# A pre-norm attention and FFN block on one core: the order of weight preparation at the start, the warming products and the power instructions

## The chip, the cores and the metric

One core of a Trainium2 chip runs the whole kernel. The metric is the device time of one execution in microseconds (us): the median before is 983.02 us of 4 runs (982.63 to 983.35). In the profile, PE is TensorE (PEld its weight loads), DVE is VectorE, ACT is ScalarE, POOL is GpSimd and SP is SyncE, which issues most DMAs. Each engine takes its own instructions in a fixed order; a wait at the head of an engine's queue holds all that stands behind it.

## The reference

Inputs are `x` of 8 x 512 x 256 floats, `gamma` (256), `w_qkv` (256 x 3072), `w_out` (1024 x 256), a router matrix (256 x 8) and the two FFN matrices (256 x 1024 and 1024 x 256) with biases. There are 16 heads of 64. Cut to what matters:

```python
xn  = rms_norm(_layernorm(x), gamma)          # x / norm * sqrt(256) * (gamma + 1)
q, k, v = split(xn @ w_qkv)                   # per head
attn = softmax((q * 64 ** -0.5) @ k.T)
x = x + (attn @ v) @ w_out
y = _layernorm(x)
combine = top-2 of softmax(y @ router_w), normalised
x = x + (gelu(y @ w1 + b1) @ w2 + b2) * sum(combine)
```

## The kernel before, in words

**Numbers in two halves.** Products run in 16-bit floats, but nearly to float accuracy: every operand is stored as a high part (the value cast to f16) and a low part (value minus high part, also f16), and every product is three products: high by high, low by high, high by low (`PARTS`, line 462). For weights, `split` (line 166) does this: ACT writes `hi` as a Copy with a scale factor, then DVE writes `lo` with one `scalar_tensor_tensor`. The scale factor is a power of two times `gamma + 1`. It is found from the weights themselves: ACT squares a weight tile with an accumulator (`square`, line 174), TensorE adds over the partitions with a matrix of ones (`total`, line 186, the tile `pn`), and DVE makes a power of two from the sum with shifts (`powers`, line 201); `with_gamma` (line 224) multiplies it by `gamma + 1`. For q and k, `find_qk` (line 231) returns `rest`, seven more small DVE instructions that give `ab`, the factors with which QT and KT are scaled after their product. The weights come as halves of 512 columns: q0, k0, v0, v1, q1, k1. 128 columns belong to a pair of heads, so that q0 and k0 hold the pairs 0 to 3.

**Start (lines 717 to 756).** x of the first batch element, gamma and the weights are loaded (lines 130 to 140); q1 and k1 go into the pool `stage` of four buffers, which the first four halves fill, so that SP waits for two of these to be read. TensorE runs 80 products of zeros (`warm`, line 720) from the start on. DVE finds the mean and variance of x, POOL raises to the powers -0.5 and 0.5 (`scale1`, lines 382 to 401), DVE normalises the four row tiles (`normalize`, line 413). ACT squares q0, k0 and v0; then come `pn`, the factors, the split of all 512 columns of q0 and k0, the transposes of the normalised x (`transpose_rows`, line 426; the tile `xnT`), `rest`, the squares of v1, and the projection of pair 0 (`project_qk`, line 490; the tile `pqk`), which ACT and DVE turn into QT and KT.

**Steps (lines 958 to 979).** A tile of scores is 128 rows of one pair of heads against all 512 keys: 256 such tiles in all, four for each pair, 8 pairs for each batch element. The loop goes over 128 double steps of two tiles each, so that a batch element takes 16. In each: TensorE makes the scores `ps` (`scores`, line 517); DVE takes the row maximum `mx`; ACT runs the exponential, four instructions `e<-ps`; ACT casts the high part `hl`; POOL subtracts the low part; SP issues a DMA that transposes both into `hT`; three double steps later (`LAG = 6` tiles) TensorE multiplies `hT` by VT (`weigh`, line 557; the tile `po`) and DVE divides (`divide`, line 577). Other work is put into the double steps by a table, `at(step, position, function, arguments)` (line 763): position "d" stands after the maxima and before the exponentials (and one step later than its number says), "a" makes a product whose high and low parts come after the exponentials, "e" comes after the exponentials and ahead of the parts of "a", "b" comes at the end of the step. Every second double step projects the next pair (QT and KT), the others make a tile of v (VT). The split of v (`split_wv`) stands in steps 0 and 1, the squares of q1 and k1 in "d" of step 1, their factors in step 3, their split (`split_qk1`) in steps 4 and 5, loads and squares of `w_out` and the router in steps 2 to 6, and their split in steps 11 to 16. `scale1`, `scale1_rest`, `scale1_last` and `normalize` for the next batch element stand in "d", on POOL but for a reciprocal. The order on each engine is as written out here.

After the attention of the last batch element come the FFN products of all elements (lines 984 to 1021); the change doesn't touch them.

Two lines that the steps of the prediction turn on:

```python
wqk = [const.tile([P, NC, 2, INNER], F16, name=f"wqk{i}") for i in range(2)]   # high and low parts of q and k
lows = [part_qk("q", 0, c) for c in range(NC)]                                 # c: the two halves of 128 input rows
```

Of the kernel before, what the change touches and what calls it, by code (L numbers as in the profile page):

```python
# [11 lines left out]
F32 = mybir.dt.float32  # L12
# [5 lines left out]
ALU = mybir.AluOpType  # L18
# [11 lines left out]
VW = 130  # L30
WARM = 80
EARLY = 6
HLB, HTB = 5, 7
SB = 4
XB = 4
# [41 lines left out]
def preln_block(  # L77
# [45 lines left out]
    def staged(name, src, eng, shape=(NC, 512)):  # L123
        t = stage.tile([P, *shape], F32, tag="stage", name=name)
        eng.dma_start(out=t, in_=src)
        return t
# [7 lines left out]
    for name, off, eng in (  # L134
        ("q0", 0, nc.scalar), ("k0", INNER, nc.sync), ("v0", 2 * INNER, nc.sync),
        ("v1", 2 * INNER + 512, nc.sync), ("q1", 512, nc.sync), ("k1", INNER + 512, nc.sync),
    ):
        raw[name] = staged(f"w_{name}", wqkv_r[:, :, off : off + 512], eng)
    for b in range(1, XB):
        load_x(b)  # L140
    w_r = const.tile([P, NC, NE], F32, name="w_r")
# [23 lines left out]

    def split(hi, lo, src, f):

        nc.scalar.activation(hi, src, AF.Copy, scale=f)
        return lambda: nc.vector.scalar_tensor_tensor(lo, src, f, hi, ALU.mult, ALU.subtract)
# [4 lines left out]
    def square(name, col, src, scale=1.0):  # L174

        pool, what = (hl_p, "hT") if name in ("qk0", "v") else (stage, "stage")
        junk = pool.tile([P, 1024], BF16, tag=what, name="junk", bufs=HTB if what == "hT" else SB)
        nc.scalar.activation(
            junk[:, 0 : src.shape[-1]], src, AF.Square, scale=scale,
            accum_out=sums[name][:, col[0], col[1] : col[1] + 1],  # L180
        )
# [41 lines left out]

    def with_gamma(name, s):

        f = stat.tile([P, 2, NC], F32, name=f"f_{name}")
        for i in range(2):
            nc.vector.tensor_scalar(f[:, i, :], gam1, s[:, i : i + 1], None, ALU.mult)
        return f

    def find_qk(half, n2):

        v = nc.vector
        added(n2)
        s, u, z = powers(f"qk{half}", n2)
        factors["qk", half] = with_gamma(f"qk{half}", s)

        def rest():  # L240
            ab = stat.tile([P, 2], U32, name=f"ab_{half}")
            w = stat.tile([P, 1], U32, name=f"w_{half}")
            v.tensor_copy(w, u[:, 1:2])
            v.tensor_tensor(z[:, 0:1], u[:, 0:1], w, ALU.add)
            v.tensor_scalar(z[:, 0:1], z[:, 0:1], 101, 254, ALU.add, ALU.min)
            v.tensor_scalar(w, z[:, 0:1], 1, None, ALU.logical_shift_right)
            v.tensor_tensor(u[:, 0:1], z[:, 0:1], w, ALU.subtract)
            v.tensor_scalar(ab[:, 0:1], u[:, 0:1], 23, None, ALU.logical_shift_left)
            v.tensor_scalar(ab[:, 1:2], w, 23, None, ALU.logical_shift_left)
            factors["out", half] = ab.bitcast(F32)  # L250

        return rest

    def find_v(n2):
        added(n2)
        s, u, z = powers("v", n2)
        factors["v"] = with_gamma("v", s)
        factors["1/v"] = inverses("v", u, z)
# [29 lines left out]
    with ExitStack() as att:  # L288
# [13 lines left out]
        VT = [work.tile([P, HEADS, VW], F16, tag=f"VT{r}", name=f"VT{r}") for r in range(NT)]  # L302

        wv = [work.tile([P, NC, INNER], F16, name=f"wv{i}") for i in range(2)]
        wo = [work.tile([P, NP, D], F16, name=f"wo{i}") for i in range(2)]
# [11 lines left out]

        def part_qk(n, half, c):
            i = "qk".index(n)
            hi, lo = (w[:, c, i, ts(half, 512)] for w in wqk)  # L320
            return split(hi, lo, raw[f"{n}{half}"][:, c], factors["qk", half][:, i, c : c + 1])

        def squares(name, i, key):
            for c in range(NC):
                square(name, (i, c), raw[key][:, c, :], gam1[:, c : c + 1])

# [9 lines left out]
        def split_qk1(n, c):  # L336
            part_qk(n, 1, c)()
            done("wqk")

        def split_wv(c, j):  # L340
            cols = ts(j, 512)
            f = factors["v"][:, j, c : c + 1]
            split(wv[0][:, c, cols], wv[1][:, c, cols], raw[f"v{j}"][:, c, :], f)()
            done("wv", j)
# [36 lines left out]

        def scale1(b, part):


            g = nc.vector if b == 0 else nc.gpsimd
            mv = norm1[b][0]
            if part == 0:
                rstd = tiny.tile([P, NT], F32, tag="rstd", name="rstd")
                g.tensor_scalar(rstd, mv[:, :, 1], LN_EPS, None, ALU.add)
                nc.gpsimd.tensor_tensor(rstd, rstd, halves[:, 0, :], ALU.pow)  # L390
                nm = tiny.tile([P, NT], F32, tag="nm1", name="nm1")
                g.tensor_scalar(nm, mv[:, :, 0], -1.0, None, ALU.mult)
                norm1[b] += [nm, rstd]
                return
            norm = tiny.tile([P, NT], F32, tag="norm", name="norm")
            g.tensor_scalar(norm, mv[:, :, 1], float(D), 1e-30, ALU.mult, ALU.max)
            nc.gpsimd.tensor_tensor(norm, norm, halves[:, 1, :], ALU.pow)
            _, nm, rstd = norm1[b]
            g.tensor_tensor(norm, norm, rstd, ALU.mult)
            g.tensor_scalar(norm, norm, NORM_EPS, float(D) ** -0.5, ALU.max, ALU.mult)  # L400
            norm1[b] = [nm, None, norm, rstd]
# [11 lines left out]
        def normalize(norm, b, t, tag):  # L413
# [5 lines left out]
            c = slice(t, t + 1)  # L419
            eng = nc.vector if (tag, b) == ("x", 0) else nc.gpsimd  # L420
            src = (xs if tag == "x" else x2)[b]
# [4 lines left out]
        def transpose_rows(b, c):  # L426

            if c == 0:
                xnT[b] = work.tile([P, NC, 2, S], F16, tag="xnT", bufs=2, name=f"xnT{b}")
            pt = bank("pt")  # L430
            need(NT, "xn", "x", b)
# [58 lines left out]
        def project_qk(pair, n):  # L490

            b, p = divmod(pair, NP)
            need(NC, "xnT", b)
            if p >= NP // 2:
                need(2 * NC, "wqk")
            pm = bank("pqk")
# [222 lines left out]

        warm = bank("warm")  # L720
        for i in range(WARM):
            nc.tensor.matmul(warm[:, 0:256], cold[:, 0:P], cold, start=True, stop=True)

# [5 lines left out]
        nc.vector.tensor_scalar_add(gam1, gam, 1.0)  # L729
        scale1(0, 0)  # L730
        scale1(0, 1)
        for name, k, m in (("qk0", 2, NC), ("v", 2, NC), ("qk1", 2, NC), ("o", 3, 1), ("w", 3, 2)):
# [5 lines left out]
        for t in range(NT):  # L738
            normalize(norm1, 0, t, "x")
        squares("v", 0, "v0")  # L740
        rest = find_qk(0, total("qk0"))
        parts = [transpose_rows(0, c) for c in range(NC)]
        lows = [part_qk("q", 0, c) for c in range(NC)]
        for high, _ in parts:
            high()
        lows += [part_qk("k", 0, c) for c in range(NC)]
        for _, low in parts:
            low()
        for low in lows:
            low()  # L750
        rest()
        squares("v", 1, "v1")
        for high, low in [project_qk(0, n) for n in range(2)]:
            high()
            low()
        lows = [find(find_v, "v")[1]]

# [36 lines left out]

        for c in range(NC):
            at(0, "e", split_wv, c, 0)
            at(1, "e", split_wv, c, 1)
            at(4, "e", split_qk1, "q", c)
            at(5, "e", split_qk1, "k", c)
        for i in range(2):  # L800
            at(1, "d", squares, "qk1", i, "qk"[i] + "1")
        at(3, "b", find_rest, find_qk, 1, "qk1")
        at(2, "d", load_small)
        for j in range(2):
            at(3 + j, "d", load_wo, j)
            at(5 + j, "d", square_wo, j)
        at(5, "d", square_wr)
        at(10, "b", find, find_o, "o")
# [12 lines left out]
        for b in range(B):  # L821
# [10 lines left out]
            if b + 1 < B:  # L832
                at(max(s0 - 5, 1), "d", scale1_rest, b + 1)
                at(s0 - 4 if b else 2, "d", scale1_last, b + 1)
                for t in range(NT):
                    at(s0 + 21 + 2 * t, "a", project, b, 1, t)
                    at(max(s0 - 9 + t // 2, 0), "d", sums1, b + 1, t)
                    at(s0 + (1 + t if b else 2 + t // 2), "d", normalize, norm1, b + 1, t, "x")
                at(max(s0 - 7, 0), "d", scale1, b + 1, 0)
                at(max(s0 - 6, 0), "d", scale1, b + 1, 1)  # L840
                if b + XB < B:
                    at(s0 + 33, "d", load_x, b + XB)
                for c in range(NC):
                    at(s0 + 6 + 2 * c, "b", transpose_rows, b + 1, c)
        del units[-2, "a"]
# [210 lines left out]
```

## Time and profile before

The profiled execution took 982.73 us; its span in the profile, from the first instruction to the last, is 980.6 us.

| What | us |
|---|---|
| median of 4 runs | 983.02 |
| the profiled execution | 982.73 |
| its span | 980.6 |
| squares of q0 and k0 begin on ACT (q0 has landed) | 8.11 |
| last warming product begins | 12.11 |
| `f_qk`, the factors of q0 and k0, ready | 14.31 |
| first product `pqk` of pair 0 | 16.79 |
| QT of pair 0 on ACT | 21.13 |
| first exponential, double steps 0, 1, 2, 3 | 25.00, 32.33, 41.99, 48.27 |
| double steps 4, 5, 6 | 52.44, 62.08, 70.35 |
| double steps 11, 16 | 100.41, 132.03 |

A row of the timeline has the start, the time from the start of the first to the end of the last of its instructions, the engine, the operation, what is written and read, and how many instructions are merged; in brackets the idle time of the engine before it and what ended that. Instructions of one engine overlap a little: of two in a row, the second starts before the first has wholly ended, so that the distance from start to start is smaller than one instruction's time. PEclk is the share of its full clock that TensorE was granted.

### The profile page before, as it was taken

What the parts mean: (1) busy time and instruction counts of PE and PEld (TensorE: products, weight loads), DVE (VectorE), ACT (ScalarE), POOL (GpSimd) and SP (SyncE); (2) the same over time, 40 slices, a digit from 0 to 9 for tenths busy, and PEclk for the clock granted to TensorE, in tenths of its full rate; (3) what the DMA queues carried; (4) which work ended last, traced back from release to release, by engine and by line L of the source; (5) the groups of instructions that cost most, each with busy time, mean ns of one, the idle gap of its engine ahead of it and who ended that gap; (6) DMA issues with size and microseconds to landing.
All of it is one profiled execution on the core that took longest, in us unless ns stands there. A gap on an engine that the chain in (4) does not pass through costs nothing.

```text
span 980.6 us, 27892 instructions
## 1 busy us (share of the span) xinstructions
PE 944.8 (96%) x11290; PEld 604.7 (62%) x11290; DVE 716.4 (73%) x1298; ACT 848.8 (87%) x1275; POOL 689.9 (70%) x717
## 2 busy tenths in 40 slices
PE   7789999989999999999999999999999999999998
PEld 5345566656666666665666666666666666666666
DVE  5878877867788778777877787777877855665654
ACT  4989899989998999899999999999999986767772
POOL 1677878787878788888887888877798962443400
PEclk9999999999999999999999999999999999999999
DMA  4699999999999999999999999999999990333111
GB/s 159 143 186 175 171 171 177 207 204 198 190 197 200 195 205 190 205 193 206 191 197 194 196 190 174 184 187 175 191 178 187 184 188 15 89 65 93 46 48 38
DMA packets 566865, 161.35 MB, mean 165 GB/s; under 512 B 551760, under 2 KB 563152, under 8 KB 566736
## 3 DMA queue, kind: packets, MB, share of 16 engines
q1 hardware_dynamic: 565616, 156.68, 91.5%
q0 software_dynamic: 576, 2.10, 0.7%
q8 instruction: 89, 1.46, 0.6%
q10 hardware_dynamic: 544, 0.79, 0.2%
q14 instruction: 40, 0.33, 0.1%
HBM read 14.82 MB, written 6.29 MB: 22 GB/s over the span
## 4 chain that ended last, share of the span: by engine, by line
PE 51%; DVE 18%; ACT 16%; DMA 6%; issue 4%; POOL 3%; ACTq 0%; SPq 0%; POOLq 0%
ACT e L48 11%; PE pf L48 9%; PE po L48 8%; PE ps L48 8%; PE ph L48 7%; PE pqk L48 7%; DVE mx L48 7%; DMA hT<-hl 6%; PE pp L48 5%; PE pv L48 4%; POOL hl L48 3%; DVE QT L48 2%; DVE O L48 2%; DVE KT L48 2%; DVE VT L48 2%
## 5 line engine op out<-in xcount | busy, mean ns | idle before, releaser
L48 POOL TENSOR_TENSOR hl<-e,hl 128x512 f16<-128x512 f32 x512 | 576.7, 1158 | 151.7 <-issue 99.3
L48 ACT ACTIVATE e<-ps,mx 128x512 f32<-128x512 f32 x512 | 310.1, 690 | 53.0 <-DVE mx L48 47.0
L48 DVE TENSOR_REDUCE mx<-ps 128x2 f32<-128x1024 f32 x256 | 300.4, 1214 | 4.1 <-PE ps L48 3.9
L48 ACT CAST hl<-e 128x1024 f16<-128x1024 f32 x256 | 259.9, 1081 | 4.1 <-DMA hT<-hl 4.1
L48 PEld LDWEIGHTS <-hT 128*128 128x128 f16 x6144 | 204.2, 97 | 38.8 <-DMA hT<-hl 7.1
L48 PE MATMUL po<-VT,hT 128*128 128x65 f16 (+1 forms) x6144 | 209.6, 193 | 7.1 <-DMA hT<-hl 5.9
L48 PE MATMUL ps<-KT,QT 64*128 64x512 f16 x1536 | 192.7, 380 | 11.4 <-ACT e L48 9.4
L48 PE MATMUL pqk<-xnT,wqk 128*128 128x512 f16 x768 | 179.9, 385 | 7.1 <-DVE VT L48 3.7
L48 PEld LDWEIGHTS <-wqk 128*128 128x128 f16 x768 | 70.7, 99 | 111.9 <-issue 34.6
L48 PEld LDWEIGHTS <-QT 64*128 64x128 f16 x1536 | 67.5, 94 | 90.6 <-issue 27.6
L48 DVE SCALAR_TENSOR_TENSOR QT<-pqk,ab,QT 128x512 f16<-128x512 f32 x64 | 47.9, 749 | 68.0 <-ACT QT L48 68.0
L48 PE MATMUL pp<-wo,OT 128*128 128x256 f16 x768 | 95.0, 273 | 1.5 <-DVE QT L48 1.4
L48 DVE SCALAR_TENSOR_TENSOR h<-h,s_w,h 128x512 f16<-128x512 f32 x64 | 49.7, 778 | 63.9 <-ACT h L48 63.9
L48 DVE TENSOR_TENSOR VT<-pv,VT 128x512 f16<-128x512 f32 x64 | 43.9, 689 | 71.6 <-ACT VT L48 71.6
L48 PE MATMUL pv<-wv,xnT 128*128 128x512 f16 x384 | 93.3, 379 | 2.1 <-DVE QT L48 1.5
L48 PEld LDWEIGHTS <-OT 128*128 128x128 f16 x768 | 70.4, 98 | 34.7 <-issue 17.3
L48 PE MATMUL ph<-yT,w1s 128*128 128x512 f16 x384 | 89.5, 379 | 0.1
L48 PE MATMUL pf<-w2s,h 128*128 128x256 f16 x768 | 88.4, 273 | 0.0
L48 ACT ACTIVATE h<-ph,b,si_w 128x512 f32<-128x512 f32 x64 | 49.3, 771 | 41.7 <-PE ph L48 41.6
L48 PEld LDWEIGHTS <-h 128*128 128x128 f16 x768 | 75.1, 98 | 14.5
L48 PEld LDWEIGHTS <-xnT 128*128 128x128 f16 x384 | 37.3, 98 | 37.3 <-issue 4.5
L48 PEld LDWEIGHTS <-w1s 128*128 128x128 f16 x384 | 37.0, 98 | 36.8 <-issue 0.3
(129 smaller groups left out, 852.1 us busy)
## 6 DMA issues: line engine op xcount, KB each, us to landing
hT<-hl SPq DMA_TRANSPOSE x256, 5.1
w<-in_L_ffn_w_dram SPq DMA_DIRECT2D x8, 512.0 KB, 5.2
out_dram<-res SPq DMA_DIRECT2D x32, 128.0 KB, 1.7
x<-in_L_attn_x_dram SPq DMA_DIRECT2D x7, 512.0 KB, 5.5
x<-x POOLq DMA_DIRECT2D x4, 512.0 KB, 5.9
x2s<-x SPq DMA_DIRECT2D x4, 512.0 KB, 3.5
w_k<-in_L_attn_w_qkv_dram SPq DMA_DIRECT2D x2, 512.0 KB, 6.1
w_v<-in_L_attn_w_qkv_dram SPq DMA_DIRECT2D x2, 512.0 KB, 8.1
```

Of the source, the lines that this page charges most:

```text
L48: i = method(*args, **kw)
```

## The change

- The 80 warming products become three sets: 54 at the start, 12 after the transposes of x, 8 after the projection of pair 0. They and the transposes of the first element now use PSUM tiles of the scores' pool.
- q0 and k0 are split in pieces: the 128 columns of pair 0 first, then those of pair 1, then the other 256; the low parts of pair 1 come after QT and KT of pair 0, those of the last 256 columns at the start of double step 0. `rest` stands between the low parts of q and those of k.
- `with_gamma` runs on ACT, as two scaled copies, and is called apart from `powers`.
- `scale1` writes both inputs of the powers into one tile and raises them with one POOL instruction of 128 x 8; it takes one place in the table, where it had two.
- Of the four row tiles of the first x, POOL normalises the first two.
- q1 and k1 are loaded as four pieces into buffers of the tile `OT`, not of `stage`; the loads of x1 to x3 come behind them.
- Squares: v0 and v1 are squared after the factors of q0 and k0; the first of q1 before double step 0, the second in it, those of k1 in steps 1 and 2, with their junk output in buffers of `hT`; those of `w_out` two steps later and the router's three steps later than before.
- The split of v1 goes to steps 2 and 3; statistics, scale and normalisation of the second x go to later steps, its transposes to steps 8 and 9.

```diff
-WARM = 80
+WARM = 54, 12, 8
...
-        ("v1", 2 * INNER + 512, nc.sync), ("q1", 512, nc.sync), ("k1", INNER + 512, nc.sync),
+        ("v1", 2 * INNER + 512, nc.sync),
...
-    def with_gamma(name, s):
-
-        f = stat.tile([P, 2, NC], F32, name=f"f_{name}")
+    powers_of = {}
+
+    def with_gamma(*key):
+
+        f = stat.tile([P, 2, NC], F32, name="f_" + "".join(map(str, key)))
+        s = powers_of[key if len(key) > 1 else key[0]]
+        factors[key if len(key) > 1 else key[0]] = f
         for i in range(2):
-            nc.vector.tensor_scalar(f[:, i, :], gam1, s[:, i : i + 1], None, ALU.mult)
-        return f
+            nc.scalar.activation(f[:, i, :], gam1, AF.Copy, scale=s[:, i : i + 1])
...
+        for name, off in (("q1", 512), ("k1", INNER + 512)):
+            raw[name] = []
+            for c in range(NC):
+                t = work.tile([P, 512], F32, tag="OT", name=f"w_{name}", bufs=8)
+                nc.sync.dma_start(out=t, in_=wqkv_r[:, c, off : off + 512])
+                raw[name].append(t)
+        for b in range(1, XB):
+            load_x(b)
...
-        def part_qk(n, half, c):
+        def part_qk(n, half, c, cols=slice(0, 512), eng=nc.scalar):
             i = "qk".index(n)
-            hi, lo = (w[:, c, i, ts(half, 512)] for w in wqk)
-            return split(hi, lo, raw[f"{n}{half}"][:, c], factors["qk", half][:, i, c : c + 1])
+            hi, lo = (w[:, c, i, ts(half, 512)][:, cols] for w in wqk)
+            src = raw[f"{n}{half}"][c][:, cols]
...
+            return split(hi, lo, src, factors["qk", half][:, i, c : c + 1], eng)
...
-        def scale1(b, part):
+        def scale1(b):
...
+            both_p = tiny.tile([P, 2, NT], F32, tag="norm", name="norm")
+            g.tensor_scalar(both_p[:, 0, :], mv[:, :, 1], LN_EPS, None, ALU.add)
+            g.tensor_scalar(both_p[:, 1, :], mv[:, :, 1], float(D), 1e-30, ALU.mult, ALU.max)
+            nc.gpsimd.tensor_tensor(both_p, both_p, halves, ALU.pow)
...
-            eng = nc.vector if (tag, b) == ("x", 0) else nc.gpsimd
+            eng = nc.vector if (tag, b) == ("x", 0) and t >= NT // 2 else nc.gpsimd
...
-        squares("v", 0, "v0")
         rest = find_qk(0, total("qk0"))
+        with_gamma("qk", 0)
         parts = [transpose_rows(0, c) for c in range(NC)]
-        lows = [part_qk("q", 0, c) for c in range(NC)]
+        warm_up(WARM[1])
+        squares("v", 0, "v0", [0])
         for high, _ in parts:
             high()
-        lows += [part_qk("k", 0, c) for c in range(NC)]
+        cols = slice(0, P)
         for _, low in parts:
             low()
-        for low in lows:
+        wq, wk = [[part_qk(n, 0, c, cols) for c in range(NC)] for n in "qk"]
+        cols = slice(P, 2 * P)
+        next_lows = [part_qk(n, 0, c, cols) for n in "qk" for c in range(NC)]
+        for low in wq:
             low()
         rest()
-        squares("v", 1, "v1")
-        for high, low in [project_qk(0, n) for n in range(2)]:
+        for low in wk:
+            low()
+        squares("v", 0, "v0", [1])
+        squares("v", 1, "v1", [0])
+        pairs = [project_qk(0, n) for n in range(2)]
+        warm_up(WARM[2])
+        for high, low in pairs:
             high()
             low()
-        lows = [find(find_v, "v")[1]]
+        squares("v", 1, "v1", [1])
+        squares("qk1", 0, "q1", [0])
+        for low in next_lows:
+            low()
+        cols = slice(2 * P, 4 * P)
+        last_lows = [part_qk(n, 0, c, cols) for n in "qk" for c in range(NC)]
...
+            if c == 0:
+                at(0, "e", with_gamma, "v")
+                at(4, "e", with_gamma, "qk", 1)
             at(0, "e", split_wv, c, 0)
-            at(1, "e", split_wv, c, 1)
+            at(2 + c, "e", split_wv, c, 1)
...
-        for i in range(2):
-            at(1, "d", squares, "qk1", i, "qk"[i] + "1")
+        at(-1, "d", start_v)
+        at(-1, "d", take_last)
+        at(-1, "d", squares, "qk1", 0, "q1", [1])
+        at(0, "d", squares, "qk1", 1, "k1", [0])
+        at(1, "d", squares, "qk1", 1, "k1", [1])
...
-            at(5 + j, "d", square_wo, j)
-        at(5, "d", square_wr)
+            at(7 + j, "d", square_wo, j)
+        at(8, "d", square_wr)
...
-                at(max(s0 - 7, 0), "d", scale1, b + 1, 0)
-                at(max(s0 - 6, 0), "d", scale1, b + 1, 1)
+                at(s0 - 6 if b else 3, "d", scale1, b + 1)
```

## The prediction

> **What bounds the kernel now.** I read the page's busy shares first, then the engines' timelines of the first 120 us, then the start of every double step (the first `e<-ps` of each four; e(d) below).
>
> ```profile
> span 980.6 us, 27892 instructions
> ...
> PE 944.8 (96%) x11290; PEld 604.7 (62%) x11290; DVE 716.4 (73%) x1298; ACT 848.8 (87%) x1275; POOL 689.9 (70%) x717
> ```
>
> TensorE is busy for 96% of it, so what can be gained lies where all engines wait for each other. Steady double steps last alternately 6.21 and 5.39 us; a batch element of 16 takes 93.0 (the seventh) to 95.8 us from the third on, the second 99.1, the first 107.0, and before it lie 25.0 us of start. All that the change touches, save one POOL instruction per element, lies in these first 132 us. The ACT timeline there, then DVE's:
>
> ```profile
> 12.27 0.19 ACT L48 ACTIVATION_READ_ACCUMULATOR junk<-w_v,gam 128x1 f32 x1
> 14.21 1.33 ACT L48 ACTIVATE wqk<-w_q,f_qk 128x512 f16<-128x512 f32 x2 [1.75 <-DVE f_qk L48]
> ...
> 18.95 0.19 ACT L48 ACTIVATION_READ_ACCUMULATOR junk<-w_v,gam 128x1 f32 x1
> 21.13 0.69 ACT L48 ACTIVATE QT<-pqk,ab 128x512 f16<-128x512 f32 x1 [1.99 <-DVE ab L48]
> 21.71 0.68 ACT L48 ACTIVATE KT<-pqk,ab 128x512 f16<-128x512 f32 x1
> 25.00 0.69 ACT L48 ACTIVATE e<-ps,mx 128x512 f32<-128x512 f32 x1 [2.61 <-DVE mx L48]
> ```
>
> ```profile
> 17.25 1.40 DVE L48 SCALAR_TENSOR_TENSOR wqk<-w_q,f_qk,wqk 128x512 f16<-128x512 f32 x2
> 18.57 1.41 DVE L48 SCALAR_TENSOR_TENSOR wqk<-w_k,f_qk,wqk 128x512 f16<-128x512 f32 x2
> 19.90 0.15 DVE L48 COPY w<-pn 128x1 uint32<-128x1 uint32 x1
> ...
> 54.14 2.18 DVE L48 TENSOR_SCALAR f_qk<-gam,s_qk 128x2 f32<-128x2 f32 x2
> ```
>
> ACT is idle for 1.75, 1.99 and 2.61 us: for the factors, for `ab`, for the first maximum. DVE is behind each: four full low parts (2.7 us) stand ahead of `ab`, though pair 0 needs a quarter of their columns. And the sums of q0 and k0 were done at 11.05 (the accumulator row at 10.86, 0.19 long), but `pn` waits until 12.38 behind the 80 warming products. From e(0) on, ACT and DVE hand work to each other, and a piece on either between e and the next maximum lengthens the step.
>
> **The change part by part.** Pitch is start to start, from merged rows: (x2 time minus one). ACT: scaled Copy of 512 columns 0.61 (1.33 less 0.72), e 0.58, CAST of VT, xnT, OT 0.47, QT or KT 0.57, hl 0.94, square with its read 0.70. DVE: low part 0.66, xnT or VT low 0.60, mx 1.14 (1.21 long), a chained small instruction 0.20. A successor on another engine starts about 0.04 after the end.
>
> Fewer warming products: of the 80, those after the 23rd start every 0.109 us, so 54 end at about 9.5, and `pn` follows the sums: 11.1 to 11.45 rather than 12.50, a gain of 1.05. TensorE is then idle 1.6 us, and again 1.5 us between the second set (12 x 0.109, to 13.8) and the first `pqk` at 15.2. The clock row sets the bound for that:
>
> ```profile
> 15.50:16.00 0.50, 0.00 (x0) 1.00 0.00 0
> 16.00:16.50 0.50, 0.00 (x0) 0.60 0.00 0
> 16.50:17.00 0.50, 0.21 (x1) 0.50 0.00 0
> ```
>
> TensorE was idle from 13.43, and the granted clock halved at about 16.2, after 2.8 us; two spells of 1.6 I cost at nothing, with 1.7 us at the other end (rival 1).
>
> Both powers in one POOL instruction: 128x4 took 1.03 and 1.01. The new one has 8 columns: 1.03 if all is fixed cost, 2.04 if none is; I take 1.9, since the plain 128x4 product took only 0.20. It ends at 8.8, four chained DVE instructions make it 9.6, and the four rows are scaled two on DVE (0.33 each) and two on POOL (0.55 to 1.0 each): by 10.7, at worst 11.7. The transposes (0.97) then end by 12.7, and ACT wants them at 13.9: this cover of 1.2 us hides it. Beside POOL's products `f_qk` took 2.18 us at 54.14, with POOL idle 0.36 at 13.95. The Trainium skill bears on that: VectorE: DVE Perf Modes says that a one-source operation within SBUF reads over both ports (section Mode 2x_2P), and that the second is shared with GpSimd (section Two Vector instructions with no wait between them), which speaks against scaling on both engines at once; by it the four scalings would run one after another, which changes no term of the sum, as 11.7 already holds that.
>
> Factors on ACT: two instructions of 0.20 (128x1) to 0.31 us (128x16), pitch 0.13; they take ACT 0.26 each time and free DVE of 0.36, 0.36 and 2.18. ACT now waits for `s_qk` itself, and behind the wait stand a square of v, xnT's casts and all pieces; DVE and TensorE wait for these.
>
> Small pieces: 128 columns on ACT, between 0.15 (a quarter of 0.61) and 0.31; a line through 128x16 (0.31 long, pitch some 0.21) and 512 (0.61) gives 0.31, and 0.41 for 256. The 4 full splits of 2.45 become 8 x 0.31 + 4 x 0.41 = 4.1 us of ACT; the range for that growth is 0 to 2.5. On DVE in the same way 0.27 and 0.40: 3.8 for 2.65.
>
> Squares elsewhere: v's move from ahead of the factors to behind; two of qk1's four go ahead of e(0), the others into steps 1 and 2, where four stood together before e(2) (2.8 us); wo's go from steps 6 and 7 to 8 and 9, router's from 6 to 9. The junk of qk1's takes buffers of `hT`; no transpose of the first three steps waits for one.
>
> Loads of q1 and k1 no longer wait for staging buffers, so SP issues them and x1 to x3 by about 10 rather than at 18.7 to 21.5. Every 512 KB ahead on SP's queue took about 1.3 us to follow the last, so they land by about 19; the first transpose is issued after 31. Cost nothing.
>
> Now the queues in order. `s_qk` is ready 1.41 after `pn` (as from 12.50 to 13.91): 12.86. ACT: factors to 13.16, one square to 13.87, xnT to 14.81, four pieces of pair 0 to 16.05, four of pair 1 to 17.3, two squares to 18.7. DVE: xnT's low parts 14.46 to 15.68, q's lows to 16.22, `ab` 7 x 0.17 to 17.4, k's lows to 17.96; TensorE ends pair 0 by 18.4. So QT starts when ACT is free, at 18.70 (21.13 before), KT 19.28. Then two squares, four pieces of 256 columns (1.66) and one square: ACT is free at 23.6. DVE: QT and KT low to 20.74, four lows of pair 1 to 21.8, mx to 23.04. e(0) is at 23.6, gain 1.4: the gain of 2.4 is partly spent on work brought forward.
>
> e(1): ACT runs e (2.3) to 25.95, factors, two wv pieces to 27.5, QT and KT to 28.6, two hl to 30.5, a square to 31.2. DVE has `s_v` at 25.5 (1.4 after mx), two more small ones, four half lows to 27.4, wv's to 28.8, QT and KT lows to 30.1, mx to 31.3. e(1) at 31.35 for 32.33: gain 1.0.
>
> e(2): ACT has e to 33.7, three VT to 35.1, two hl to 37.0, one square to 37.7; mx is ready at 37.3. 37.7 for 41.99, gain 4.3: three squares fewer stand there. e(3): e to 40.0, then DVE in turn: wv low to 41.4, QT, KT and VT lows to 43.4, mx to 44.6; 44.6 for 48.27. e(4): e to 46.9, wv's other half (ACT 47.7, DVE 48.4), reciprocal and product 0.5, mx 50.1; 50.15 for 52.44, gain 2.3. e(5): `s_qk` 52.5, `ab` 53.7, two lows to 55.0, QT and KT lows 56.3, 0.5, mx 58.1; 58.15 for 62.08, gain 3.9: DVE no longer stands 2.18 at the factors. e(6): e to 60.5, two pieces to 61.7 and their lows to 62.6, two VT lows 63.8, 0.5, mx 65.5; 65.6 for 70.35, 4.8, of which one square of wo and the router's (1.3) are only postponed. Steps 6 to 10 then take 6.2, 6.2 (5.39 with a square of 1.06, ACT bound), 7.1 (xnT, a square, the router's), 5.65 and 6.2: 31.4, where before they took 100.41 - 70.35 = 30.06. e(11) is at 97.0 for 100.41: gain 3.4 us. From e(11) on, both kernels hold the same instructions but for the powers: POOL saves 0.1 to 1.1 us per element, under 4.5 us of products in steps of 5.4 to 6.2; counted as nothing.
>
> The profiled execution took 982.73, 0.3 below the median of 983.02; the span of 980.6 becomes 977.2, the median 979.6. Costlier or free pieces (+0.8, -1.7 in ACT's queue) and one wait more or less in e(3) to e(6) (1 us) make its own range 977.6 to 981.
>
> **The rivals.** 1, the clock falls in the idle spells: products of 512 columns then start every 0.427 rather than 0.216 us, as from 16.79 to 19.3 before. Twelve of pair 0 end 1.7 us later, DVE waits, ACT uses 0.8 of it: about 980.5 to 981.3. For it: fewer warming products; against: 1.6 is under 2.8.
>
> 2, the gain is given back: ACT fills up. The squares, pieces and factors it takes on delay hl, whose transposes must land before the product three steps later; or the dense steps 3 to 9 wait for these. ACT then pays its extra 1.7 + 0.8 us in full and only `pn` and the 2.18 remain, less the postponed 1.3: about 982.3, no change. Against: transposes land about 15.5 us after their e, and are needed after 17.
>
> 3, slower: the whole of scale1 now stands in one POOL step before hl's low parts (before: 1.6 and 1.9 us in two steps; the timeline at 194.59 to 202.55 shows both). With a power of 2.04 it takes 3.2, up to 1.3 more ahead of hl. Where the transposes already land late (20.8 us after e at 203.7, the step of 7.86), each us reaches the products; in all seven elements 7 x 1.3 = 9.1, less 3.4: 988.7; with half, 984.2. It decides from 0.5 us each on. Against: in the sixth and seventh elements, which split no weights, the steps there last 5.39 to 5.67 and 6.21, so that nearly all of its 3.5 us is hidden now.
>
> **How the numbers follow.** 0.2% (about what a measurement can tell from no change) is 2 us: faster is below 981.05. Forecast 0.66, rival 1 0.11, rival 2 0.12, rival 3 0.11. Most of rival 1 is faster still: faster 0.76, same 0.14, slower 0.10. The range reaches into rival 2: 977.0 to 982.4; the likeliest's own is 977.6 to 981.
>
> **What would show it.** `pn` ends near 11.45 and `s_qk` near 12.9; QT starts near 18.7 with ACT busy before it, not waiting for `ab`; e(0) near 23.6, e(2) near 37.7, e(6) near 65.6, e(11) near 97.0; the granted clock stays full from 9 to 20 us; batch elements two to eight take as long as before. Wrong would be: QT after 20, e(11) within 1 us of 100.4, or later elements longer by over 0.5 us each.

## The result, and the profile after

The changed kernel takes 984.25 us (median of 29 runs, 981.03 to 988.64) where the kernel before, in runs beside it, takes 982.46 (48 runs): a ratio of 1.0016, with a 95% interval of 1.0008 to 1.0023. It is slower by 0.16%; the forecast was 979.6, faster by 0.35%. The profiled execution took 984.09, its span is 982.1.

First the page after, then ACT's timeline of the start, in the same columns as before:

```profile
span 982.1 us, 27883 instructions
...
PE 944.9 (96%) x11284; PEld 605.3 (62%) x11284; DVE 717.7 (73%) x1298; ACT 850.9 (87%) x1289; POOL 685.9 (70%) x711
```

```profile
11.90 0.48 ACT L48 ACTIVATE f_qk<-gam,s_qk 128x2 f32<-128x2 f32 x2 [1.89 <-DVE s_qk L48]
...
13.94 0.70 ACT L48 ACTIVATE wqk<-w_q,f_qk 128x128 f16<-128x128 f32 x2
...
17.69 0.68 ACT L48 ACTIVATE QT<-pqk,ab 128x512 f16<-128x512 f32 x1
18.26 0.68 ACT L48 ACTIVATE KT<-pqk,ab 128x512 f16<-128x512 f32 x1
...
22.54 1.25 ACT L48 ACTIVATE e<-ps,mx 128x512 f32<-128x512 f32 x2
```

The three idle spells of ACT that the prediction began with are now one; from 11.90 to e(0) it is busy. So the start did what it was meant to do. The starts of the first exponentials show how far the gain got (a step's time is from its e to the next one's):

| | before | forecast | after |
|---|---|---|---|
| e(0) | 25.00 | 23.6 | 22.54 |
| e(2) | 41.99 | 37.7 | 36.56 |
| e(4) | 52.44 | 50.15 | 49.12 |
| e(6) | 70.35 | 65.6 | 64.56 |
| e(11) | 100.41 | 97.0 | 98.08 |
| e(32) | 231.1 | | 227.7 |
| e(48) | 326.4 | | 327.4 |
| step 10 | 6.21 | 6.2 | 8.27 |
| step 45 | 6.29 | as before | 11.53 |
| steps 24 to 31 together | 51.97 | as before | 51.70 |

The kernel is 3.4 us ahead at e(32) and 1.0 behind at e(48): 4.4 us are lost in a stretch where the change touches nothing but POOL's powers. Step 45 alone is 5.24 longer; the other fifteen steps together are 0.8 shorter. DVE's timeline there, then POOL's:

```profile
306.56 0.17 DVE L48 TENSOR_SCALAR pn<-pn 128x3 uint32<-128x3 uint32 x1
306.77 0.16 DVE L48 TENSOR_SCALAR si_w<-pn 128x3 uint32<-128x3 uint32 x1
306.96 5.40 DVE L48 TENSOR_TENSOR f_w<-si_w 128x1 f32<-128x1 f32 x1
312.29 0.47 DVE L48 SCALAR_TENSOR_TENSOR x<-pp,f_o,x 128x256 f32<-128x256 f32 x1
```

```profile
303.26 4.49 POOL L48 TENSOR_TENSOR hl<-e,hl 128x512 f16<-128x512 f32 x4
307.72 0.19 POOL L48 TENSOR_TENSOR norm<-norm 128x4 f32<-128x4 f32 x1
307.87 4.48 POOL L48 TENSOR_TENSOR hl<-e,hl 128x512 f16<-128x512 f32 x4
```

One product of a single column, `f_w` (in `find_w`, for the FFN's weights; two columns of `si_w` multiplied), takes 5.40 us. It ends at 312.36, with POOL's last product at 312.35. The small DVE instructions before it, beside the same POOL products, took 0.16 to 0.17 each; they read PSUM (`pn`), while both operands of `f_w` are in SBUF. The same place in the kernel before:

```profile
311.21 0.16 DVE L48 TENSOR_TENSOR f_w<-si_w 128x1 f32<-128x1 f32 x1
```

```profile
310.87 0.19 POOL L48 TENSOR_TENSOR norm<-norm,rstd 128x4 f32<-128x4 f32 x1
311.76 3.38 POOL L48 TENSOR_TENSOR hl<-e,hl 128x512 f16<-128x512 f32 x3 [0.71 <-ACT hl L48]
```

There POOL had caught up with ACT and waited 0.71 us for the next high part; `f_w` fell into that pause. In the changed kernel `scale1` stands in one step: it takes POOL 3.74 us (295.02 to 298.76, a DMA issue of 0.67 among it) ahead of eight products, where the second part alone took 2.69 before (299.21 to 301.90) at the same place. So POOL is about 1.1 us later, behind ACT for these eight products and the four that follow, and does not pause.

### The profile page after: what moved, and what is told of

Read it like the earlier page. It is cut to its first block, busy times and chain, and to the rows that moved or that the text cites. A ratio compares the mean times of both kernels' runs of the same rounds, so it can differ in the third digit from the quotient of the medians.

```text
span 982.1 us, 27883 instructions
## 1 busy us (share of the span) xinstructions
PE 944.9 (96%) x11284; PEld 605.3 (62%) x11284; DVE 717.7 (73%) x1298; ACT 850.9 (87%) x1289; POOL 685.9 (70%) x711
## 3 DMA queue, kind: packets, MB, share of 16 engines
HBM read 14.82 MB, written 6.29 MB: 22 GB/s over the span
## 4 chain that ended last, share of the span: by engine, by line
PE 56%; DVE 17%; ACT 17%; issue 5%; DMA 4%; POOL 2%; ACTq 0%; POOLq 0%
ACT e L48 10%; PE po L48 9%; PE ps L48 9%; PE pqk L48 9%; PE pf L48 9%; PE ph L48 7%; DVE mx L48 7%; PE pp L48 5%; PE pv L48 4%; DMA hT<-hl 4%; DVE O L48 2%; POOL hl L48 2%; DVE QT L48 2%; DVE VT L48 2%; DVE KT L48 2%
```

## The experiments

All kernels below ran beside the kernel before; the ratio of each is to that kernel, and its median stands beside. Theory A is that `f_w` waits out POOL's unbroken run; rival T is that POOL's fuller step delays the low parts of hl and with them the transposes, as rival 3 had it.

**1. f_w on ACT.**

```diff
-        v.tensor_tensor(f, si[:, 1:2], si[:, 2:3], ALU.mult)
+        nc.scalar.activation(f, si[:, 1:2], AF.Copy, scale=si[:, 2:3])
```

> The changed kernel with one 128x1 product moved: f_w = si x w from DVE to ACT (a Copy scaled by a column), as it took 5.40 us on DVE at 306.96 while POOL ran without a pause, 0.16 in the kernel before. Theory A (this one instruction gives the start's gain back): step 45 lasts about 6.3 us instead of 11.53, the start keeps its gain, e(48) near 322.5, median 984.25 - 5.2 = about 979.0 (978.5 to 980.0), faster than before by 0.3 to 0.4%. Rival T (POOL's longer step makes the transposes of hT land late, and DVE waits for the same thing in any case): the 5 us reappear in step 45 to 47, median 983.5 to 984.5.

981.51, ratio 0.9988 (0.9979 to 0.9998), above the 978.5 to 980.0 expected. Step 45 fell from 11.53 to 5.38, but step 44 rose from 6.21 to 9.78. ACT's timeline of this run:

```profile
306.41 0.29 ACT L48 ACTIVATE f_w<-si_w 128x1 f32<-128x1 f32 x1 [4.12 <-DVE si_w L48]
306.61 2.40 ACT L48 ACTIVATE e<-ps,mx 128x512 f32<-128x512 f32 x4
```

ACT waits 4.12 us for `si_w`, and all four exponentials stand behind. The edit took one wait away and put another of 3.6 us in its place.

**2. The powers in two steps again.** From the third element on, `scale1` has its two parts and its two places as before.

```diff
-                at(s0 - 6 if b else 3, "d", scale1, b + 1)
+                if b:
+                    at(s0 - 7, "d", scale1, b + 1, 0)
+                    at(s0 - 6, "d", scale1, b + 1, 1)
+                else:
+                    at(3, "d", scale1, b + 1)
```

> The changed kernel with the two powers of every element from the third on in two steps again, as before the change (the second element keeps the single power). Theory A: POOL then has less ahead of hl's products in the step where f_w stands, f_w ends within about 1 us, and the median falls to 979 to 980. Rival T: other steps lose the time as well, and the median stays within 1 us of 984.2. A third possibility, that f_w happens to fall into POOL's products all the same: f_w takes over 2 us and the median is 981 to 984.

979.51, ratio 0.9958 (0.9945 to 0.9970). `f_w` took 0.16 us: it was issued at 305.27, as a product of POOL ended (305.30) and a pause of 0.53 began. Step 45 lasted 6.83. Undoing this one part of the change takes the whole loss away.

**3. One power alone, in the kernel before.** Its `scale1` is the changed kernel's; nothing else.

```diff
-                at(max(s0 - 7, 0), "d", scale1, b + 1, 0)
-                at(max(s0 - 6, 0), "d", scale1, b + 1, 1)
+                at(max(s0 - 6, 0), "d", scale1, b + 1)
```

> The kernel before with the one power of 128x8 alone, in one step for every element. Theory A: POOL runs about 3.2 us of small instructions ahead of hl's products in one step instead of two, and if f_w falls into that run it takes up to 5 us: step 45 up to 5 us longer, median 984 to 988; if f_w is issued at another time than in the changed kernel it takes 0.2 us and the median is 982.5 +- 0.7. Rival T (late transposes in every element): each of the later elements longer by 0.3 us or more, median above 984.5 with f_w still short.

987.40, ratio 1.0043 (1.0031 to 1.0056). DVE, then POOL:

```profile
309.24 5.40 DVE L48 TENSOR_TENSOR f_w<-si_w 128x1 f32<-128x1 f32 x1
```

```profile
310.00 0.19 POOL L48 TENSOR_TENSOR norm<-norm 128x4 f32<-128x4 f32 x1
310.14 4.48 POOL L48 TENSOR_TENSOR hl<-e,hl 128x512 f16<-128x512 f32 x4
```

The same 5.40, the same step of 11.53, again ended with POOL's run (314.64 and 314.62). Steps 24 to 31 took 50.79, less than before: no sign of rival T.

**4. The control: f_w on ACT in the kernel before.** The edit of the first experiment.

> The kernel before with f_w on ACT, the control of the first: there f_w took 0.16 us on DVE, so that nothing is to be gained. Theory A and rival T alike: 982.5 +- 0.5, ratio 0.9995 to 1.0005. If it is faster by over 1 us, the edit brings something by itself that has nothing to do with the 5.40 us.

985.76, ratio 1.0029 (1.0018 to 1.0040): a miss of mine, and what explains the first experiment. Step 44 is 9.78 here too; where there was no 5.40 to take away, only the new wait is left.

**5. One operand of f_w from PSUM.** It stays on DVE and at its place.

```diff
-        v.tensor_tensor(f, si[:, 1:2], si[:, 2:3], ALU.mult)
+        v.tensor_copy(m[:, 2:3], si[:, 2:3])
+        v.tensor_tensor(f, si[:, 1:2], m[:, 2:3], ALU.mult)
```

> The changed kernel with one operand of f_w read from PSUM: si's third column is copied there first (one more small DVE instruction), f_w stays on DVE at its place, and ACT gets no wait. Theory A, sharpened (DVE's instruction with two operands in SBUF waits out POOL's unbroken run; one with an operand in PSUM does not, as pn<-pn,b_w took 0.17 us beside POOL's products): f_w takes 0.16 to 0.20 us in the midst of POOL's products, step 45 lasts about 6.3 us, median 984.25 - 5.2 = 979.0 (978.0 to 980.0). Rival P (any DVE instruction at that place waits for POOL, or the instruction waits for something else): the copy or f_w takes over 4 us and the median stays at 983.5 to 985. Rival D (something else takes the 5 us, as ACT did in the first experiment, where e stood behind f_w on ACT's queue): f_w short, median above 981.5.

979.64, ratio 0.9964 (0.9952 to 0.9975). DVE, then POOL:

```profile
306.99 0.16 DVE L48 COPY pn<-si_w 128x1 f32<-128x1 f32 x1
307.19 0.15 DVE L48 TENSOR_TENSOR f_w<-si_w,pn 128x1 f32<-128x1 f32 x1
```

```profile
302.17 5.61 POOL L48 TENSOR_TENSOR hl<-e,hl 128x512 f16<-128x512 f32 x5
307.75 0.19 POOL L48 TENSOR_TENSOR norm<-norm 128x4 f32<-128x4 f32 x1
```

In the midst of POOL's run, with no pause near, the product takes 0.15 us. So it is not DVE that stands still beside POOL, nor POOL's step that costs: with only one operand in SBUF this instruction does not wait. Step 45 is 6.60, and the median is the forecast's.

A second operand in SBUF does not by itself mean a wait until POOL pauses. In experiment 3, where `f_w` takes 5.40, two other DVE instructions with two SBUF tensors, the low parts of a piece of the router's weights and of `w_out`, fall into a run of eight POOL products. POOL, then DVE:

```profile
107.31 9.45 POOL L48 TENSOR_TENSOR hl<-e,hl 128x512 f16<-128x512 f32 x8
```

```profile
108.60 1.01 DVE L48 SCALAR_TENSOR_TENSOR wr<-w_r,s_o,wr 128x16 f16<-128x16 f32 x1
...
110.11 1.13 DVE L48 SCALAR_TENSOR_TENSOR wo<-w_o,s_o,wo 128x512 f16<-128x512 f32 x1 [0.41 <-ACT wo L48]
```

They take 1.01 (0.22 in the changed kernel) and 1.13 (0.75 earlier in this run, at 103.93). The first ends at 109.61, as the second product does (109.59), and both are done long before the run is, which takes 9.45 where eight products took 8.97 in the changed kernel (at 298.78). Why `f_w` did not get in at the end of a product, as `wr` did, is not shown: it is another operation, and both its operands lie in one tile.

**6. 80 warming products again**, on top of experiment 5.

```diff
-WARM = 54, 12, 8
+WARM = 80, 12, 8
```

> The kernel of the run before this with 80 warming products in the first set again in place of 54. The prediction's first term: pn ends 1.05 us earlier by the smaller number. If the start's waits hold that on the path: s_qk near 13.9 instead of 11.87, QT and e(0) later by 1.0 to 2.0, median 1.0 to 2.0 above the run before this. Rival: xnT's casts and the loads set the start anyway; e(0) later by under 0.5 and the median within 0.5.

981.22, ratio 0.9982 (0.9972 to 0.9992), 1.6 above experiment 5. The four sums of q0 and k0 were done at 10.18, `pn` was issued at 11.28, and e(0) came 13.47 us after the sums. With 54 products and these factors on ACT it came 12.52 to 12.55 after them in six profiles (the changed kernel's and experiments 1, 2, 8, 9 and 11) and 12.73 in experiment 5, told below: 0.94 lost. The other 0.6 of the median is within what such medians differ by.

**7. All factors on DVE again**, on top of experiment 5, in `with_gamma`:

```diff
-            nc.scalar.activation(f[:, i, :], gam1, AF.Copy, scale=s[:, i : i + 1])
+            nc.vector.tensor_scalar(f[:, i, :], gam1, s[:, i : i + 1], None, ALU.mult)
```

> The kernel with f_w from PSUM, and with the three pairs of factors (f_qk twice, f_v) on DVE again. The prediction's term: DVE is freed of 0.36, 0.36 and 2.18 us, ACT takes 0.26 each time. If that holds: f_qk of the second half takes 1 to 2.2 us on DVE near 50 us beside POOL's products, e(6) later by 1 to 2.5 us, e(0) within 0.4; median 1 to 2.5 above the kernel with f_w from PSUM. Rival: POOL pauses there now or DVE has slack: f_qk under 0.5 in all, median within 0.5.

978.92, ratio 0.9960 (0.9946 to 0.9975): no difference to experiment 5 that can be told, against an expected loss of 1 to 2.5. By parts: e(0) came 11.70 after the sums instead of 12.53, since ACT did a square of v while DVE made the factors; step 0 took 8.99 for 7.65 and step 4 8.87 for 7.99. `f_qk` of the second half took 0.22 each; the 2.18 of the kernel before does not recur at its new place (53.28), where POOL's products had ended at 52.93. Up to e(11) that is 1.4 lost, and the profile has it back in steps 24 to 31 (47.66 for 51.53), which vary from run to run.

**8. The second element's transposes of x in steps 8 and 10** instead of 8 and 9, on top of experiment 5.

```diff
-                    at(s0 + (6 + 2 * c if b else 8 + c), "b", transpose_rows, b + 1, c)
+                    at(s0 + (6 + 2 * c if b else 8 + 2 * c), "b", transpose_rows, b + 1, c)
```

> The kernel with f_w from PSUM, and with the second element's two transposes of x in steps 8 and 10 instead of 8 and 9. In the changed kernel TensorE is idle for 1.96 us at 89.3 in step 9, where O's transposes stand as well: both hold a PSUM bank until DVE has taken their low parts at 91.24, and pqk waits for a bank. In the changed kernel's profile the clock fell after that spell and step 10 took 8.27 us; in two other profiles with the same idle 1.96 it did not fall and the step took 6.71. Theory C: without the spell step 9 to 11 are shorter by 0.3 to 0.7 us and no execution loses the 1.6 us, median 0.3 to 1.0 below the kernel with f_w from PSUM. Rival: the later transpose is waited for by VT or pqk of the second element, or the idle time moves to step 10: within 0.3, or later by up to 1.

982.21, ratio 0.9990 (0.9981 to 0.9999), 2.6 worse than experiment 5. The idle 1.96 us is gone, but the low part of the later transpose now stands on DVE behind the eight small instructions of `find_o` (97.84 to 99.81), the next tile of v waits for it, and step 11 takes 9.99 for 6.24. Part of that is the clock: TensorE was idle for 3.54 us up to 100.47, the granted clock halved at 100.9, and the products `po` after it took 2.83 for 1.63. The rival was right in kind; it had allowed at most 1 us.

**9. The four first loads of the FFN weights spread out**, on top of experiment 5.

```diff
-                at(16 + 4 * n + 2 * j, "d", load_w, n, j)
-                at(20 + 4 * n + 2 * j, "d", square_w, n, j)
+                when = (16, 19, 22, 34)[2 * n - 2 + j]
+                at(when, "d", load_w, n, j)
+                at(when + 4, "d", square_w, n, j)
```

> The kernel with f_w from PSUM, and with the four first loads of w_1 and w_2 (512 KB each, for their squares) in steps 16, 19, 22 and 34 instead of 20, 22, 24 and 26, their squares four steps behind as before. Every profile so far but one loses 3 to 4 us in steps 26 to 30, in both families: the transposes land 10 to 12 us after their low parts there (4.6 in step 15), beside these loads and a write of x at 201. Theory L: it is the sum of the loads in so few steps; apart from each other they are absorbed: the lag stays under 10 us, steps 24 to 31 take about 47 us (6.21 and 5.39 in turn) instead of 51 to 54, median 975.5 to 977.5. Rival: the transposes have no slack anywhere and the same time is lost at another step: 979 to 980.5.

977.21, ratio 0.9949 (0.9936 to 0.9962). Steps 24 to 31 took 46.75 us, for 51.53 in experiment 5. The wait that this shortens is on ACT, in the group of `hl` on the page (last column: idle time before it, and what ended it); first the changed kernel, then this one:

```profile
L48 ACT CAST hl<-e 128x1024 f16<-128x1024 f32 x256 | 259.8, 1081 | 6.9 <-DMA hT<-hl 6.7
```

```profile
L48 ACT CAST hl<-e 128x1024 f16<-128x1024 f32 x256 | 260.2, 1083 | 2.4 <-DMA hT<-hl 2.3
```

This has nothing to do with the change: of the eleven profiles of both families without this edit, ten lose 3.2 to 5.6 us there against four pairs of 6.21 and 5.39 (46.4). Steps 36 to 47, to which one load moved, give back 0.7 (72.33 for 71.63).

**10. One power alone in the kernel before, with f_w from PSUM**: the edits of experiments 3 and 5.

> The kernel before with the one power of 128x8 alone (third experiment, 987.4) and f_w from PSUM. Theory A: all that the one power cost there was f_w's 5.4 us: f_w takes 0.16, step 45 about 6.3, median 982.3 to 983.3, as the kernel before. Rival T (POOL's longer step costs by itself): 984 or more.

981.65, ratio 0.9981 (0.9971 to 0.9991). `f_w` 0.16, step 45 6.61. The 4.5 us of experiment 3 are gone, and a little more: the one power by itself is not a loss, perhaps a gain of about 1 us, whose place I did not trace.

**11. Two powers, f_w from PSUM and the spread loads together**: the edits of experiments 2, 5 and 9.

> The changed kernel with all three: the two powers in two steps, f_w from PSUM, loads spread. If f_w is all that the one power cost, f_w from PSUM leaves nothing for the two powers to bring: the same as the kernel with f_w from PSUM and the loads spread, within 0.7 us. If the one power also makes the transposes late: 1 us or more below it.

979.44, ratio 0.9961 (0.9947 to 0.9975), no better than experiment 9: the medians are 2.2 apart, more than the 0.7 expected and the other way round; the profiled spans are 0.3 apart (973.8 and 973.5), and the intervals overlap. Undoing the merged power brings nothing that shows once `f_w` reads PSUM.

**12. The first factors on DVE**, those of v and of the second half on ACT, on top of experiment 9, in `with_gamma`:

```diff
-            nc.scalar.activation(f[:, i, :], gam1, AF.Copy, scale=s[:, i : i + 1])
+            if key == ("qk", 0):
+                nc.vector.tensor_scalar(f[:, i, :], gam1, s[:, i : i + 1], None, ALU.mult)
+            else:
+                nc.scalar.activation(f[:, i, :], gam1, AF.Copy, scale=s[:, i : i + 1])
```

> The kernel with f_w from PSUM and the loads spread, and with the first factors (f_qk of the first half) on DVE, those of v and of the second half on ACT as in the changed kernel. From the seventh experiment: with f_qk on DVE, ACT does a square of v while it waits for s_qk, and e(0) came 11.70 us after the last of the four sums instead of 12.53; its steps 0 and 4, where the other factors stand, were 1.34 and 0.88 longer. If these are three separate effects: e(0) 11.7 after the last sum, step 0 7.65, step 4 7.99, median 0.8 below the kernel with the loads spread (977.21): about 976.4. Rival: the 0.8 is given back in the first steps by work of ACT: within 0.4.

976.46, ratio 0.9942 (0.9924 to 0.9959). e(0) came 12.03 after the sums for 12.55, 0.5 of the expected 0.8; steps 0 and 4 are 7.65 and 7.99. It is the lowest median of all, 0.75 below experiment 9; that the two differ is not settled by their intervals. Both are faster than the kernel before and the changed one.

## Why the prediction failed, step by step

**The step that failed** is the last sentence of the change's costs: "From e(11) on, both kernels hold the same instructions but for the powers: POOL saves 0.1 to 1.1 us per element, under 4.5 us of products in steps of 5.4 to 6.2; counted as nothing." It counted POOL's time and not its pauses. What it put at nothing measured 5.24 us (step 45, 11.53 for 6.29), all of it in one DVE instruction that had lived in one of those pauses. Shown by undoing the part (2), by doing it alone (3), and by taking away the second SBUF operand at the same place (5).

A warning was in the row that the prediction itself used, `f_qk` at 54.14 with 2.18 for 0.36: two instructions of 1.06 and 1.20, which ended at 55.20 and 56.32 as products of POOL ended at 55.18 and 56.29. The prediction read this as the price of that instruction and not as a wait for POOL that other DVE instructions can meet. The Trainium skill says of whom it holds: GPSIMD Engine Reference, section Specifications, has POOL's SBUF interfaces shared with VectorE, with contention for instructions in a 2-port mode or with two SBUF inputs. Experiments 3 and 5 agree with the second half of that (5.40 with two SBUF inputs, 0.15 with one); how long such a wait lasts the page doesn't say. The runs show one product for `wr` and, for `f_w`, the rest of one product, a small one of 0.19 and four more, until POOL stopped; what decides between the two stays open.

**The start: right.** Measured from the end of the four sums, the forecast's e(0) was 23.6 - 11.05 = 12.55; the profile has 22.54 - 10.01 = 12.53. The absolute 1.06 is when the sums were done: over the profiles of both families the last read ends between 9.85 and 11.35, which is hidden in the kernel before by the 80 products (e(0) at 24.9 to 25.34) and shows after. From e(0) to e(6) the forecast was 42.0 and the profile has 42.02. The warming products' 1.05 measured 0.94 (6); the power of 128x8, taken as 1.9 of 1.03 to 2.04, took 1.66. The two scalings on POOL took 0.86, beside DVE's, and 0.55, and ended at 11.08, within the 10.7 to 11.7 foreseen.

**The factors on ACT: a gain that the times do not show.** By the profile they cost 0.8 for the first half rather than gain, since a square stands behind ACT's wait, and the other two gain 1.34 and 0.88 (7); the medians of 7 and 5 show no difference. The 2.18 us to be saved would have been 0.35 on DVE at the new place.

**Steps 6 to 10: 31.4, measured 33.5.** 1.6 of the 2.1 is rival 1 in another place. TensorE is idle for 1.96 us in step 9, until DVE has taken the low part of `OT` (91.23), one of two transposes that hold PSUM banks there, and in this execution its clock fell afterwards; the other 0.5 is step 10 as well, 6.71 without the fall where 6.2 was foreseen. A row below has a stretch and its length, the busy time of PE, PEld, DVE, ACT and POOL, the granted clock, the busy share of the DMA engines and GB/s; the changed kernel first, then experiment 2, idle for the same 1.96 us:

```profile
92.00:92.50 0.50, 0.50 (x4) 0.26 (x3) 0.00 (x0) 0.50 (x2) 0.50 (x1) 0.89 1.11 214
92.50:93.00 0.50, 0.50 (x6) 0.22 (x5) 0.10 (x1) 0.36 (x1) 0.17 (x1) 0.50 1.16 214
```

```profile
92.00:92.50 0.50, 0.50 (x4) 0.26 (x3) 0.00 (x0) 0.50 (x2) 0.50 (x1) 1.00 1.09 213
92.50:93.00 0.50, 0.50 (x14) 0.38 (x13) 0.04 (x1) 0.50 (x2) 0.41 (x2) 1.00 1.14 212
```

Step 10 took 8.27 in the one and 6.71 in the other. Of nine profiles with this idle spell three have the fall.

**The rivals.** Rival 1 was priced at 0.9 to 1.7 for the start. There the clock did fall in experiment 5, whose weights landed late (TensorE idle for 2.72 us from 8.68): e(0) came 12.73 after the sums, 0.2 later. It fell in experiment 2 too, at 11.8, though the longest idle spell before was 1.00 us (from 9.10), and e(0) came no later (12.52). So "1.6 is under 2.8" was no safeguard, and the price was too high; the row that it rests on has the fall at 16.1, 2.7 us after 13.43. Rival 2 did not happen; the gain stood at 5.8 us at e(6). Its price of 982.3 is 1.05 and 2.18 less 1.7 and 0.8; the postponed 1.3 that its sentence also subtracts is not in it. Rival 3 had the right place, `scale1` in one POOL step, and a fitting time, 984.2, by the wrong way: the transposes were no later (steps 24 to 31, 51.70 for 51.97), and the fourth to seventh element took as long as before (95.71, 95.24, 93.14 and 92.99 for 95.85, 95.17, 93.17 and 93.05).

**The time.** 979.6 was forecast and 979.64 measured for the kernel without the one wait. That closeness is partly chance: a clock fall, late weights and late transposes move single runs by 1 to 4 us.

## What to carry to other kernels

Before POOL's work is merged or moved, list the DVE instructions that read two tensors from SBUF and ask in which pause of POOL each of them runs; a product of one column can cost as much as a step, as `f_w` did, though not every such instruction waits so long. If such an instruction stands on the path, give it an operand in PSUM rather than another engine, whose queue would wait for its input. And when one group of instructions keeps its total but a step doubles, look for the instruction whose own time grew, not for what came late.

## What was not expected of the hardware

- A DVE instruction of 128x1 with two SBUF operands took 5.40 us beside POOL products of 1.15 us each that followed each other without a pause, twice to the same 0.01 us; with one operand in PSUM 0.15. In one of the same two profiles a DVE instruction of 128x16 with two SBUF operands got in after 1.01 us, at the end of one product of such a run.
- TensorE's clock halved after an idle spell of 1.96 us in three of nine profiles and not in the other six, with the same instructions around it. The Trainium skill, TensorE: Matmul & The Clock Gate, section What's actually happening, has a window that runs freely, so that the phase decides; that it falls in some profiles only agrees with this; the table there asks for at least one idle window of about 3.4 us, and here the wholly idle spell was 1.96 us.
- Four loads and one write of 512 KB between 165 and 211 us delay the transposes from 4.6 us after their low parts (step 16) to 11.3 (step 28), and ACT waits 4.19 us for them at 214.49; with the loads spread (9) steps 24 to 31 lose 0.35 us in all.
